# Moving two row normalisations of a fused attention and mixture-of-experts layer from VectorE to ScalarE

## The chip, the core and the metric

The kernel runs on one core of a Trainium2 chip. Its engines work from queues of their own and wait for each other by semaphores: TensorE (PE in the profile, PEld for its weight loads), VectorE (DVE), ScalarE (ACT), GpSimd (POOL) and SyncE (SP, which here only issues transfers). The metric is the device time of the whole kernel in microseconds (us), the median of several runs. Lower is better.

## What is computed

The input x is (2, 4096, 512) in float32: two batches of 4096 rows. The output is x plus an attention part plus a mixture-of-experts part, both fed with the normalised rows:

```python
x = L0_attn_x
xn = _layernorm(x, axis=-1)             # (x - mean) / sqrt(var + 1e-5)
x = x + attn(xn) + ffn(xn)

# attn: 64 compressed features per row, normalised again
c = (xn @ W_to_kv.T) @ W_compress.T
ch = (c - mean(c)) * rsqrt(var(c) + 1e-5) * ln_gamma + ln_beta
q, k, v = ...                           # from ch, with rotary tables
o = softmax(causal(q @ k.T / 8)) @ v
out = z @ W_to_kv + z @ W_out_res.T + b_out_res      # z = o @ W_comp2lat.T

# ffn: a shared expert for every row, and the best 2 of 16 experts per row
router_logits = xn @ router_w.T
shared = (silu(xn @ shared_gate_w) * (xn @ shared_up_w)) @ shared_down_w
```

## The kernel before

There are three phases. The first goes through the rows in 16 groups of 512 (four tiles of 128 rows each): statistics, normalisation, router logits, compressed features, the whole shared expert, the choice of experts, and every second group the projection to q, k and v. It ends near 740 us. The second gathers rows for their experts and multiplies them by the experts' weights. The third is the rest of the attention and the final sum. The change touches only the first phase.

The groups alternate between the batches: `seq` (L648) is half 0 of batch 0, half 0 of batch 1, half 1 of batch 0 and so on. A batch-1 group is followed by `project` (L608) for its half, whose work in the trace stands at the beginning of the stretch of the next batch-0 group.

For each group, in the order of the code:

- `front` (L372) belongs to the next group: it is called through `ahead` (L487, L724) in the middle of the current one. `load_x` (L360) loads 512 rows into one of two buffers. VectorE computes mean and variance (L376, L377), ScalarE the square root (L368), VectorE the reciprocal (L369), and L381 normalises four tiles of 128x512 into `xn`, which has a single buffer. POOL then adds the output bias to x in place (L384), so that the shared expert can be summed onto it.
- `group` (L450): TensorE multiplies the transposed rows into `lc`, a PSUM tile with 16 router logits and 64 compressed features per row (L458). VectorE takes the statistics of the features from PSUM (L466, L467), ScalarE the square root, and L471 normalises them into `cn` (128x64, four times). Then come the two best logits (L476, L477), the exponential for their weights (L481), and the store of `xn` with the weights in two extra columns (L488).
- The shared expert uses a scheme of seven products on quarters (`product`, L331) for gate and up together, and seven more for down. A product of gate and up fills one of two PSUM pairs. `sent(1)` is copied out by ScalarE (L517); the next ones, in the order 6, 2, 7, 5, 4, 3, are added onto running sums in SBUF by VectorE (L529, L530, L532, L534, L539, L541, L547), which frees the pair for the product after next. `gated` applies SiLU on ScalarE in place (L506) and multiplies on VectorE, both operands in SBUF (L507), into `hT`.
- The quarters of `hT` are combined for the down step (L546, L565 to L568), seven products follow in the order 1, 2, 4, 6, 7, 5, 3, and their sums go onto x (L581 to L601), which is stored (L602). Only then can the next load into that buffer start.
- `turn_x` (L430) transposes the next group's `xn` on TensorE, and ScalarE copies the result out (L447). `project` transposes `cn` and a copy of it with the batches swapped (`cns`, made by ScalarE in L621), applies gamma and beta (L626 on VectorE, L628 on ScalarE), and multiplies.

The order of instructions within each engine in this phase is not written out by hand. A planner sets it before the kernel runs, from the order of the code as a priority and from its own estimates of when inputs are ready. From the second phase on (L934) the order of TensorE, VectorE and ScalarE is that of the code.

The square root, the exponential and SiLU belong to different function tables of ScalarE. A change of table shows as an ACT_TABLE_LOAD on the line that needs it.

## Time and profile before

| | |
|---|---|
| median of three runs | 1941.44 us (1939.95, 1941.44, 1946.81) |
| profiled execution: time / span | 1946.36 / 1944.6 us |
| granted TensorE clock, mean | 0.99 |
| L381, VectorE, 64 instructions | 30.6 us, 542 ns each |
| L471, VectorE, 64 instructions | 17.6 us, 336 ns each |
| L384, POOL, 16 instructions | 76.0 us, 4752 ns each |
| ACT_TABLE_LOAD on L368, L506, L481 | 31, 23 and 16 times, 1283 ns each |

The profile is one execution, and a row of it gives a line of the code, the engine, the operation, output and input by name and shape, how often, the busy time and the mean duration. Behind a second bar stands the idle time of that engine just before these instructions and who ended it. In a timeline the two numbers ahead of the engine are start and duration in us from the start of the span, and brackets hold the idle time before. A busy engine isn't yet the one that sets the time: what sets it is who is waited for.

### The profile page before, as it was taken

What the parts mean: (1) busy time and instruction counts of PE and PEld (TensorE: products, weight loads), DVE (VectorE), ACT (ScalarE), POOL (GpSimd) and SP (SyncE); (2) the same over time, 40 slices, a digit from 0 to 9 for tenths busy, and PEclk for the clock granted to TensorE, in tenths of its full rate; (3) what the DMA queues carried; (4) which work ended last, traced back from release to release, by engine and by line L of the source; (5) the groups of instructions that cost most, each with busy time, mean ns of one, the idle gap of its engine ahead of it and who ended that gap; (6) DMA issues with size and microseconds to landing.
All of it is one profiled execution on the core that took longest, in us unless ns stands there. A gap on an engine that the chain in (4) does not pass through costs nothing. (4 is left out here: it accounts for less than half of the span.)

```text
span 1944.6 us, 33411 instructions
## 1 busy us (share of the span) xinstructions
PE 1866.0 (96%) x13010; PEld 1377.1 (71%) x13010; DVE 1060.9 (55%) x2882; ACT 648.2 (33%) x1097; POOL 575.6 (30%) x499
## 2 busy tenths in 40 slices
PE   7999999999999988999999999999999998999997
PEld 6888888888888875577777777777776674544544
DVE  8788778778787886632222222222223325777765
ACT  2222323233233324721111111111111454666664
POOL 2233433323242351011111111111111105555554
PEclk9999999999999999999999999999999999999998
DMA  6222223233222214067787887788776667888987
GB/s 238 66 77 66 76 66 94 71 94 102 66 77 66 77 49 153 2 196 262 271 301 250 271 285 275 270 277 283 272 278 236 241 221 192 206 206 208 217 208 183
DMA packets 219441, 342.52 MB, mean 176 GB/s; under 512 B 19204, under 2 KB 109952, under 8 KB 219280
## 3 DMA queue, kind: packets, MB, share of 16 engines
q1 hardware_dynamic: 167600, 234.09, 37.0%
q0 software_dynamic: 31696, 69.99, 14.3%
q10 hardware_dynamic: 19984, 36.25, 4.9%
q8 instruction: 105, 1.72, 0.4%
q14 instruction: 56, 0.46, 0.1%
HBM read 250.22 MB, written 90.05 MB: 175 GB/s over the span
## 5 line engine op out<-in xcount | busy, mean ns | idle before, releaser
L1043 PE MATMUL pg<-xt,wgu 128*128 128x256 f32 (+1 forms) x2816 | 496.1, 335 | 0.0
L1043 PEld LDWEIGHTS pg<-xt,wgu 128*128 128x128 f32 x2816 | 434.8, 191 | 43.0 <-issue 0.5
L985 POOL DMA_INDIRECT xg<-xn_d,table x137 | 130.6, 954 | 704.8 <-DVE sw L1025 553.2
L1049 DVE TENSOR_TENSOR eh<-esg,pg 128x512 f32<-128x512 f32 (+1 forms) x69 | 47.2, 683 | 396.6 <-ACT esg L1048 396.6
L1057 PE MATMUL py<-wdn,eh 128*128 128x512 f32 x548 | 247.1, 594 | 0.0
L1020 DVE COPY xt<-pxt 128x512 f32<-128x512 f32 x138 | 88.3, 681 | 176.7 <-PE pxt L1017 176.6
L1057 PEld LDWEIGHTS py<-wdn,eh 128*128 128x128 f32 x548 | 102.2, 190 | 106.6 <-issue 98.5
L812 DVE TENSOR_SCALAR_CACHE_REDUCE E<-s 128x512 f32<-128x512 f32 x224 | 144.7, 686 | 56.6 <-PE s L804 46.6
L1061 ACT ACTIVATE y<-py,sw 128x512 f32<-128x512 f32 x137 | 94.2, 688 | 231.4 <-PE py L1057 203.0
L1048 ACT ACTIVATE esg<-pg 128x512 f32<-128x512 f32 (+1 forms) x69 | 41.0, 594 | 383.1 <-PE pg L1043 292.2
L820 ACT ACTIVATE E<-E,nb 128x1024 f32<-128x1024 f32 (+7 forms) x160 | 160.8, 1008 | 22.6 <-DVE nb L815 22.5
L804 PE MATMUL s<-kT,qT 64*128 64x512 f32 (+3 forms) x576 | 145.0, 591 | 13.4 <-DVE E L812 8.7
L874 PE MATMUL oT<-eT,vv 128*64 128x256 f32 (+1 forms) x1088 | 145.7, 389 | 5.1 <-DVE qT L876 3.4
L423 POOL DMA_INDIRECT order_d<-tok,at_u x128 | 128.8, 1007 | 64.5 <-issue 36.1
L860 ACT COPY eT<-et 128x512 f32<-128x512 f32 x184 | 101.3, 587 | 111.8 <-PE et L854 84.4
L384 POOL TENSOR_TENSOR x<-x,b_bc 128x2048 f32<-128x2048 f32 x16 | 76.0, 4752 | 204.0 <-DVE xn L381 191.1
L874 PEld LDWEIGHTS oT<-eT,vv 128*64 128x64 f32 x1088 | 67.1, 137 | 94.2 <-ACT eT L860 32.1
L854 PEld LDWEIGHTS et<-ident,E 64*128 64x128 f32 x2112 | 83.5, 141 | 67.6 <-issue 47.8
L1135 POOL DMA_INDIRECT fac<-y_d,pos_all x64 | 99.8, 1560 | 72.8 <-DMA fac<-y_d,pos_all 56.8
L854 PE MATMUL et<-ident,E 64*128 64x64 f32 x2112 | 103.1, 232 | 14.0 <-ACT eT L860 6.3
L1135 POOL DMA_INDIRECT fyy<-y_d,pos_all x64 | 82.1, 1284 | 115.1 <-SPq L1090 54.6
L337 PE MATMUL gu<-xnT,Wg 128*128 128x256 f32 x384 | 99.5, 403 | 14.8 <-DVE gs L530 14.8
(246 smaller groups left out, 2728.1 us busy)
## 6 DMA issues: line engine op xcount, KB each, us to landing
wgu<-in_L_ffn_gate_w_dram SPq DMA_DIRECT2D x88, 512.0 KB, 5.5
wgu<-in_L_ffn_up_w_dram SPq DMA_DIRECT2D x88, 512.0 KB, 7.7
wdn<-in_L_ffn_down_w_dram SPq DMA_DIRECT2D x88, 512.0 KB, 4.7
y_d<-y ACTq DMA_DIRECT2D x137, 256.0 KB, 6.2
xn_d<-xn SPq DMA_DIRECT2D x16, 1028.0 KB, 7.1
x<-in_L_attn_x_dram SPq DMA_DIRECT2D x16, 1024.0 KB, 6.1
acc_d<-x SPq DMA_DIRECT2D x16, 1024.0 KB, 4.8
fac<-acc_d SPq DMA_DIRECT2D x64, 256.0 KB, 4.8
```

Of the source, the lines that this page charges most:

```text
L337: mm(out=o[:, r, :], lhsT=lhs[:, c, r * P:(r + 1) * P], rhs=rhs[:, c, :], start=c == 0, stop=c == 1)
L423: G.indirect_dma_start(out=order_d[n % 4], out_offset=bass.IndirectOffsetOnAxis(ap=at_u[:, i, k:k + 1], axis=0), in_=tok[:, g * 4 + i, k:k ...
L804: mm(out=sc[b][:, 0:w], lhsT=q[e, :], rhs=kT[c][e, 0:w], start=True, stop=True)
L812: V.tensor_scalar(dst, sc[b][:, 0:w], SCALE, None, ALU.mult, ALU.max, accum_out=m)
L820: S.activation(E, E, AF.Exp, bias=nb[:, b:b + 1], accum_out=sm[:, b, c:c + 1])
L854: tr(pt[h][:, o:o + H], rows[i][j // 8][e, b, (j % 8) * P:(j % 8 + 1) * P], ident[e, e])
L860: copy(dst[:, h:h + 3:2, :], pt[h].rearrange("p (u c) -> p u c", u=2))
L874: mm(out=o, lhsT=vv[j // 4][:, b, j % 4, :], rhs=e, start=(j == 0), stop=(j == n - 1))
L985: G.indirect_dma_start(out=x_n, out_offset=None, in_=xn_d, in_offset=bass.IndirectOffsetOnAxis(ap=table[:, n:n + 1], axis=0))
L1043: mm(out=pg[:, g, f, at_s], lhsT=weights[u][0][:, c, g * FE + f * P:g * FE + (f + 1) * P], rhs=x_u[:, c, :], start=(c == 0), stop=(c == 3))
L1057: mm(out=py[:, v, :], lhsT=hT[:, c, v * P:(v + 1) * P], rhs=weights[u][1][:, c, :], start=(c == 0), stop=(c == 1))
L1135: G.indirect_dma_start(out=y, out_offset=None, in_=y_d, in_offset=bass.IndirectOffsetOnAxis(ap=pos[k][:, j:j + 1], axis=0), compute_op=ALU ...
```

## The change

Both normalisations go from VectorE's "subtract the mean, multiply by the factor" to ScalarE's activation with the identity function, which computes factor times input plus addend. The factor is the same reciprocal as before. The addend, minus mean times factor, is a new small VectorE instruction for each group and each of the two normalisations, on 128x4 values, in a tile of its own with four buffers.

```diff
+            def minus_mean(mv, r, name):
+                m = p1.tile([P, 4], F32, tag="mmr", name=name, bufs=4)
+                V.scalar_tensor_tensor(m, mv[:, :, 0], -1.0, r, ALU.mult, ALU.mult)
+                return m
+
             def front(g, xt):
...
                 r = rstd_of(mv, 4, f"rx{g}")
                 xn = p1.tile([P, 4, D + TOPK], F32, tag="xn", name=f"xn{g}", bufs=1)
+                m = minus_mean(mv, r, f"mx{g}")
                 for i in range(4):
-                    V.tensor_scalar(xn[:, i, 0:D], xt[:, i, :], mv[:, i, 0:1], r[:, i:i + 1],
-                                    ALU.subtract, ALU.mult)
+                    S.activation(xn[:, i, 0:D], xt[:, i, :], AF.Identity, bias=m[:, i:i + 1], scale=r[:, i:i + 1])
...
                 r = rstd_of(mv, 4, f"rc{g}")
                 b = g // GPB
+                m = minus_mean(mv, r, f"mc{g}")
                 for i in range(4):
-                    V.tensor_scalar(cn[:, i, b, :], lc[:, i, NE:NE + DC], mv[:, i, 0:1], r[:, i:i + 1],
-                                    ALU.subtract, ALU.mult)
+                    S.activation(cn[:, i, b, :], lc[:, i, NE:NE + DC], AF.Identity, bias=m[:, i:i + 1], scale=r[:, i:i + 1])
```

## The prediction

> **What bounds the kernel now.** I read the page first, then busy time by stretches of 40 us, then the waits from 60 to 760 us (the first phase, which ends near 740 us), and last the timeline of two neighbouring groups. The page's totals, one stretch (us, then busy time of PE, PEld, DVE, ACT, POOL, the granted clock, DMA share, GB/s) and the waits ("total us, times, longest"):

> ```profile
> PE 1866.0 (96%) x13010; PEld 1377.1 (71%) x13010; DVE 1060.9 (55%) x2882; ACT 648.2 (33%) x1097; POOL 575.6 (30%) x499
> 440.00:480.00 40.00, 38.82 (x281) 32.68 (x280) 33.87 (x87) 13.95 (x21) 16.88 (x14) 1.00 0.22 68
> PE gu L337 <- DVE gs L530: 14.8, 7, 3.5
> PE gu L337 <- DVE gs L529: 4.2, 7, 1.0
> DVE st L376 <- DMA x<-in_L_attn_x_dram: 36.6, 14, 5.3
> ```

> The first phase is TensorE's: 38.8 of 40 us busy, VectorE 33.9, ScalarE 14.0. VectorE is heavily loaded, but what matters is how long TensorE waits for it. That is 14.8 + 4.2 = 19 us in the whole phase, always in one place: a product needs a PSUM pair that L529 or L530 frees by adding it away. The timeline of a batch-1 group (start, duration, engine) shows why L530 is late:

> ```profile
> 438.72 1.29 DVE L376 BATCH_NORM_STATS2 st<-x 128x6 f32<-128x512 f32 x2 [2.92 <-DMA x<-in_L_attn_x_dram]
> 441.32 1.19 DVE L530 TENSOR_TENSOR gs<-gs,gu 128x1024 f32<-128x1024 f32 x1
> 442.54 0.63 ACT L506 ACTIVATE gs<-gs 128x512 f32<-128x512 f32 x1 [8.43 <-DVE gs L530]
> 442.56 1.99 PE L337 MATMUL gu<-xnT,Wg 128*128 128x256 f32 x8 [1.18 <-DVE gs L530]
> 444.81 0.18 DVE L369 RECIPROCAL rx<-rx 128x4 f32<-128x4 f32 x1 [0.51 <-ACT rx L368]
> 445.03 1.91 DVE L381 TENSOR_SCALAR xn<-x,mv,rx 128x512 f32<-128x512 f32 x4
> 446.86 1.21 DVE L534 TENSOR_TENSOR gs<-gs,gu 128x1024 f32<-128x1024 f32 x1
> 447.02 4.55 POOL L384 TENSOR_TENSOR x<-x,b_bc 128x2048 f32<-128x2048 f32 x1 [15.40 <-DVE xn L381]
> 449.28 1.28 ACT L506 ACT_TABLE_LOAD   x1 [4.50 <-DVE gs L539]
> 451.24 1.49 DVE L507 TENSOR_TENSOR hT<-gs 128x512 f32<-128x512 f32 x2 [0.24 <-ACT gs L506]
> ```

> The statistics of the next rows stand in VectorE's queue ahead of L530 and wait 2.92 us for the load of x. That load waits for the same buffer's store (issued 427.00 after the last sum onto x, landed near 431.8; the load goes out at 431.90 and lands 6 to 7 us later). VectorE idles there; it isn't short of time. The normalisation itself (445.03) comes after L530, and in the batch-0 group before it (399.3 to 401.2) after L529 and L530 too.

> **What the change removes, adds and moves.** The rows (mean ns behind the bar) that carry the costs:

> ```profile
> L381 DVE TENSOR_SCALAR xn<-x,mv,rx 128x512 f32<-128x512 f32 x64 | 30.6, 542 | 7.6 <-DMA xn_d<-xn 7.3
> L471 DVE TENSOR_SCALAR cn<-plc,mvc,rc 128x64 f32<-128x64 f32 x64 | 17.6, 336 | 0.5
> L628 ACT ACTIVATE chT<-ptc,bet,gam 128x512 f32<-128x512 f32 x8 | 6.2, 778 | 9.8 <-PE ptc L623 9.8
> ```

> VectorE loses 30.6 + 17.6 = 48.2 us (1.91 and 1.10 us a group). It gains 32 small instructions for the addend; L415, the same kind on 128x8, takes 0.16 us: 5.1 us. Net -43 us of engine time, of which none is a wait of TensorE.

> ScalarE, the rows: L628 has the same function with both operands per row, from PSUM, at 0.778 us. The SiLU of L506 from SBUF takes 0.630, the copy L447 from PSUM 0.597, so I add 0.03 for the source: 0.81. Four L447 copies take 2.05 us where 4 x 0.597 = 2.39, so each after the first overlaps by 0.11: four in 2.9 us. The bounds are 2.05 us (plain copies) and 3.2 us (no overlap). The compressed rows, 128x64: the 128x4 square root with one operand per row takes 0.297; 60 more elements add 0.05 at the slope of L517 against L447 (1.00 - 0.597 us for 512); L628 against L447 gives 0.09 for an operand. That is 0.44, or 1.4 us for four. In all 16 x (2.9 + 1.4) = 69 us on an engine that is busy 14 of 40 us. [...] The time hides as follows. In the batch-1 group ScalarE sits idle from 444.79 to 449.28; reciprocal (445.0), addend (to 445.2) and four activations end near 448.2, ahead of the table load that waits for L539. In the batch-0 group it idles from 399.4 to 406.7; the rows end near 402.3. Transposes first need the rows near 421.9 and 464: cost 0, and if the cover is gone the 2.9 us stand ahead of a SiLU. For the compressed rows, cn would be ready near 431.5; if it goes ahead of the copy L517 (431.11), that copy ends at about 433.9 instead of 432.1, and product 2 needs its PSUM pair at 434.09 in batch 1 (covered) and at 392.4 in batch 0 (where the copy would end at 392.8: 0.4 us). I take it behind the copy: 0; bound 7 x 0.4 = 3 us. The store of xn waits for the exponential, which is ready before cn: SP's queue isn't moved. Table loads: L628 is issued today between functions of three tables without one on its line, so none is added; the bound, if every group loaded one more, is 16 x 1.28 us on ScalarE, inside its idle time.

> The wait of up to 1.5 us that L381 makes for the store of the old rows (7.3 us over 7 groups) passes to ScalarE; behind it is then a SiLU due 7 us later. Nothing of TensorE waits for it today.

> What moves is L384 on POOL, which overwrites x and so must now follow ScalarE: from 447.0 to about 448.3, ending at 452.9 instead of 451.6. Its own result isn't needed for 20 us. [...]

> The start: ScalarE can take the first rows from about 11.7 us (reciprocal 11.39), while VectorE begins only at 13.27 behind L314 and the evacuation L690. 11.7 + 2.9 = 14.6 against 15.18: -0.5 us. By the other bound (it starts when VectorE did) it is +1.2. The last group has no next rows; its cn, behind the copy L517 (to 697.1), would end near 698.5, before the transposes at 699.7: 0.

> **Sum.** -0.5 for the start, 0 to +3 for the compressed rows (I take +0.5), 0 for the rest: 0 us. The profiled execution has a span of 1944.6 us and a time of 1946.36, 4.9 above the median of the runs, 1941.44; I carry the difference over to the median and forecast 1942. About 0.5%, 9.7 us, is what a measurement of this kernel can tell from no change.

> The order within each engine's queue in this phase is the planner's; it may change with the cost of the moved work, and that I can't see in this trace. All rivals stand on it.

> **Rivals.** *Faster: the 19 us close.* With cn gone and rows off the queue the planner may put L529 or L530 ahead of the statistics. For it: those sums are ready at 392.4 and 439, before the statistics are done. Against: what holds them is the load of x, which the change doesn't touch. Half to all of 19 us, with some granted clock (0.91 to 0.96 in four stretches): about -12, 1929. Chance 0.18.

> [...] Chance 0.22.

> *Slower: a SiLU behind rows that wait for a store.* In batch 0 the rows wait for the old rows' store until 399.3; ahead of the SiLU they would hold it until 402.3, then table load and L507 in front of L532, which must end by 404.06 and would end near 406. 2 us in 7 groups: +14, 1956. Against: the SiLU's sum L530 is done before the reciprocal. Chance 0.10.

> *No change that can be told:* my forecast, chance 0.50.

> **Numbers.** Faster by over 0.5% 0.18, within 0.5% 0.51, slower 0.31 (nearly all of the two slower cases). The range runs from 1929 to 1963: it holds half of the faster case, the second slower case and the lock in 7 groups with some in the others; the far half of the one (0.09) and the lock in most groups (0.08) are left out. My forecast's own range is 1936 to 1948: the 3 us bounds above, and the spread of the runs (6.9 us).

> **What would show it.** Right: VectorE's busy time some 43 us lower, ScalarE's some 69 higher, the waits of products for L529 and L530 still near 19 us, stretches of 40 us still with about 39 of TensorE. [...] A SiLU held shows as L507 waiting for L506 (11.0 us in 27 waits now). Closed gaps show as the L530 row gone. Wrong I am if the planner's order is another, first of all the order of the statistics, L529 and L530.

## The result and the profile after

The changed kernel takes 1972.45 us (median of six runs), the kernel before 1942.55 us beside it: a ratio of 1.0156, 95% interval 1.0138 to 1.0173. It is 30 us slower, where the prediction said 1942 us and a range of 1929 to 1963 us. Of the two slower rivals, the SiLU behind the rows at 1956 us and VectorE's product held by POOL's addition at 1958 us, both are found in the trace, in the same seven groups.

The profiled execution took 1971.71 us. From the page of the changed kernel, and from its waits between 60 and 780 us (engine, line, what it waited for: total us, times, longest us). Five lines were added, so L381 of before is now L387, L506 and L507 are L511 and L512, the sums L529, L530 and L539 are L534, L535 and L544, and the bias addition L384 is L389.

```profile
PE 1872.1 (95%) x13010; PEld 1379.2 (70%) x13010; DVE 1045.0 (53%) x2786; ACT 712.7 (36%) x1225; POOL 568.2 (29%) x499
...
L389 POOL TENSOR_TENSOR x<-x,b_bc 128x2048 f32<-128x2048 f32 x16 | 72.4, 4527 | 236.8 <-ACT xn L387 224.0
```

```profile
PE gu L337 <- DVE gs L544: 16.4, 7, 2.8
PE gu L337 <- DVE gs L535: 12.6, 7, 3.4
PE gu L337 <- DVE gs L534: 8.7, 7, 2.9
...
ACT xn L387 <- DMA xn_d<-xn: 25.0, 7, 3.8
...
DVE hT L512 <- ACT gs L511: 26.8, 30, 2.8
```

TensorE's waits for sums grew from 19 to 37.7 us. One row is new: the wait for L544 (product 5's second sum, behind which the pair is free for product 3), once in each of the seven batch-0 groups behind the first step. L534 rose from 4.2 to 8.7, L535 changed little. Two other waits have grown with it: ScalarE stands idle for 25.0 us ahead of the normalised rows until the store of the old rows has landed (VectorE for 7.3 us), and `hT` waits 26.8 us for the SiLU (11.0). VectorE's wait for the load of x grew too, from 36.6 to 47.1 us.

Where it lies is seen from the time between the first transpositions of two groups. A step that holds a batch-0 group took 45.55 us in the mean and now takes 49.96 us (seven steps; the first step, with the start in it, is left out); one with a batch-1 group took 43.92 and takes 43.26 us. The last group's first transposition moves from 686.87 to 714.37 us, so the whole loss is there by then. The sums of TensorE's busy time over these 15 steps, of the kernel before and of the changed one:

```profile
sum 673.00, PE 653.29 PEld 556.83 DVE 533.43 ACT 203.35 POOL 232.87; mean PE 43.55 PEld 37.12 DVE 35.56 ACT 13.56 POOL 15.52
```

```profile
sum 700.14, PE 661.61 PEld 560.25 DVE 517.75 ACT 265.94 POOL 227.65; mean PE 44.11 PEld 37.35 DVE 34.52 ACT 17.73 POOL 15.18
```

The steps are 27.1 us longer. Idle time of TensorE is 18.8 us of that (38.5 against 19.7), and 8.3 us are busy time: the same matmuls took longer. About half of the 8.3 us is the granted clock: TensorE worked 13.0 us at a clock of 0.50 in these steps before and 21.8 us after. In the kernel before, 8 matmuls take the 3.00 us from 353.0 at a clock of 0.50 and 16 the 3.00 us from 356.5 at 1.00, so half of the difference is lost, 4.4 us. For the rest the traces give only an estimate: a step at full clock is busy for 40.61 us without a wait (in the kernel before with late statistics, at the end of the experiments) and for 40.88 us with one (in the kernel before, 151.13 to 193.22), so seven more waits make some 1.9 us. The last 2 us are open.

The timeline of one batch-0 group of the changed kernel shows the chain (start, duration, engine):

```profile
405.68 0.17 DVE L369 RECIPROCAL rx<-rx 128x4 f32<-128x4 f32 x1
...
405.96 1.22 DVE L535 TENSOR_TENSOR gs<-gs,gu 128x1024 f32<-128x1024 f32 x1
...
408.44 2.93 ACT L387 ACTIVATE xn<-x,mx,rx 128x512 f32<-128x512 f32 x4 [3.47 <-DMA xn_d<-xn]
...
411.39 1.28 ACT L511 ACT_TABLE_LOAD   x1
411.45 4.53 POOL L389 TENSOR_TENSOR x<-x,b_bc 128x2048 f32<-128x2048 f32 x1 [11.84 <-ACT xn L387]
...
412.68 0.63 ACT L511 ACTIVATE gs<-gs 128x512 f32<-128x512 f32 x1
...
413.35 3.18 DVE L512 TENSOR_TENSOR hT<-gs 128x512 f32<-128x512 f32 x1 [2.55 <-ACT gs L511]
...
416.45 1.21 DVE L539 TENSOR_TENSOR gs<-gs,gu 128x1024 f32<-128x1024 f32 x1
417.58 1.21 DVE L544 TENSOR_TENSOR gs<-gs,gu 128x1024 f32<-128x1024 f32 x1
...
418.93 1.97 PE L337 MATMUL gu<-xnT,Wg_s 128*128 128x256 f32 x8 [2.49 <-DVE gs L544]
```

It is read from top to bottom. The SiLU's input is ready at 407.2 (L535). But on ScalarE the rows stand ahead of it, and ScalarE is idle for 3.47 us until the store of the old rows has landed (the addend is there at 406.04, so the store alone holds the rows for 2.4 us). Then come 2.93 us of rows and 1.28 us of table load, and the SiLU runs at 412.68, 5.5 us after its input was there. By now the end of the rows has also released POOL's bias addition at 411.45. VectorE's product L512 comes at 413.35, in the middle of it, and takes 3.18 us instead of 0.69: it ends 0.55 us behind the addition (416.53 and 415.98). This hold is called the lock here, and the expectations below call it the port or the port lock; what the two engines share isn't shown by any run. Two sums stand behind it on VectorE, and TensorE waits 2.49 us for the second.

In the kernel before, the same place has another order: on ScalarE the table load comes at 397.43 and the SiLU at 398.73, while the rows wait for the store in VectorE's queue:

```profile
397.43 1.28 ACT L506 ACT_TABLE_LOAD   x1
398.73 0.63 ACT L506 ACTIVATE gs<-gs 128x512 f32<-128x512 f32 x1
...
399.27 1.91 DVE L381 TENSOR_SCALAR xn<-x,mv,rx 128x512 f32<-128x512 f32 x4 [0.86 <-DMA xn_d<-xn]
```

### The profile page after: what moved, and what is told of

Same layout as the page of the kernel before. It is cut to its first block, busy times and chain, and to the rows that moved or that the text cites. A ratio compares the mean times of both kernels' runs of the same rounds, so it can differ in the third digit from the quotient of the medians.

```text
span 1969.9 us, 33487 instructions
## 1 busy us (share of the span) xinstructions
PE 1872.1 (95%) x13010; PEld 1379.2 (70%) x13010; DVE 1045.0 (53%) x2786; ACT 712.7 (36%) x1225; POOL 568.2 (29%) x499
## 5 line engine op out<-in xcount | busy, mean ns | idle before, releaser
L389 POOL TENSOR_TENSOR x<-x,b_bc 128x2048 f32<-128x2048 f32 x16 | 72.4, 4527 | 236.8 <-ACT xn L387 224.0
L337 PE MATMUL gu<-xnT,Wg 128*128 128x256 f32 x384 | 99.1, 402 | 12.6 <-DVE gs L535 12.6
```

Of the source, the lines that this page charges most:

```text
L337: mm(out=o[:, r, :], lhsT=lhs[:, c, r * P:(r + 1) * P], rhs=rhs[:, c, :], start=c == 0, stop=c == 1)
```

## The experiments

Twelve kernels ran, four at a time on one chip. The kernel before took 1955.14 us on the first of these chips, 1960.82 us on the second and 1944.09 us on the third; so only ratios to the runs of before on the same chip are compared, and "of before" below means these. Steps and waits come from one profile of each kernel and differ a little between chips too: a batch-0 step of the change took 49.96 us, and 50.41 us on the second of these chips. My theory after the result was: rows ahead of the SiLU on ScalarE, then VectorE's product held by POOL's addition, both needed. The rivals: the wait for the store alone, the lock alone, ScalarE's added work as such, and one half of the change by itself.

**The SiLU ahead of the rows.** The rows and the bias addition are listed behind the first SiLU of a group; all else is as changed.

```diff
-                for i in range(4):
-                    S.activation(xn[:, i, 0:D], xt[:, i, :], AF.Identity, bias=m[:, i:i + 1], scale=r[:, i:i + 1])
+                def rows():
+                    for i in range(4):
+                        S.activation(xn[:, i, 0:D], xt[:, i, :], AF.Identity, bias=m[:, i:i + 1], scale=r[:, i:i + 1])
+                    G.tensor_tensor(xt, xt, b_bc.unsqueeze(1).to_broadcast([P, 4, D]), ALU.add)
 
-                G.tensor_tensor(xt, xt, b_bc.unsqueeze(1).to_broadcast([P, 4, D]), ALU.add)
+                if g == seq[0]:
+                    rows()
+                else:
+                    held_back.append(rows)
...
-                    gated(k1, 0, 0)
+                    with tc.issue_after(gated(k1, 0, 0).ins):
+                        held_back.pop()()
```

> The changed kernel, but the activations of the rows are queued behind the first SiLU of the group on ScalarE (a queue order, no wait). Theory (two delays in series in the batch-0 groups: the SiLU stands behind rows that wait 3.6 us for the store of the old rows, and then POOL's addition of the bias holds the port when L512 comes): the SiLU is early again, L512 of 3.2 us is gone, product 3 waits no longer for L544 (16.4 us in 7 waits now). About 17 us less than the changed kernel, 1955. Rival (the port lock alone): L512 is still held somewhere, since POOL still starts when the rows end, 1968 to 1972. Rival (more work on ScalarE as such, or VectorE's new order): no gain, 1972.

Measured: a ratio of 1.0026 (1.0006 to 1.0045). Steps with a batch-0 group take 46.52 us, against 49.96 in the change and 45.55 before, and TensorE's waits for sums in the first phase are those for the first two, as before:

```profile
PE gu L337 <- DVE gs L542: 14.2, 7, 3.8
PE gu L337 <- DVE gs L541: 9.3, 7, 1.6
```

(L541 and L542 are L534 and L535 of the change.) The row for product 5's sum is gone, and the product that was held takes its usual time in the same group:

```profile
399.94 0.69 DVE L518 TENSOR_TENSOR hT<-gs 128x512 f32<-128x512 f32 x1 [0.69 <-ACT gs L517]
```

1.3 of the 1.56 per cent hang on this order, more than the 17 us I had expected. The same work is on the same engines. But two things were moved together, the rows and, with them, POOL's addition.

**The store early.** The rows are stored as soon as they are made, and the two weight columns from a small tile of their own, so that the next rows find their buffer free.

```diff
+                nc.sync.dma_start(
+                    out=xn_d[g * 512:(g + 1) * 512, 0:D].rearrange("(i p) d -> p i d", p=P), in_=xn
+                )
                 return (xn,)
...
-                V.tensor_copy(xn[:, :, D:D + 1], ww)
-                V.tensor_tensor(xn[:, :, D + 1:D + 2], dl, ww, ALU.mult)
+                wt = p1.tile([P, 4, TOPK], F32, tag="wt", name=f"wt{g}")
+                V.tensor_copy(wt[:, :, 0:1], ww)
+                V.tensor_tensor(wt[:, :, 1:2], dl, ww, ALU.mult)
                 nxt = ahead()
                 nc.sync.dma_start(
-                    out=xn_d[g * 512:(g + 1) * 512, :].rearrange("(i p) d -> p i d", p=P), in_=xn
+                    out=xn_d[g * 512:(g + 1) * 512, D:].rearrange("(i p) d -> p i d", p=P), in_=wt
                 )
```

> The changed kernel, but the rows are stored as soon as they are normalised, and the two weight columns go out of a small tile of their own, so that the next rows never wait for a store. Theory: ScalarE's 25 us of waits for the store are gone, rows, SiLU and POOL's addition all come 2 to 3 us earlier in batch 0; L512 is still held by the port, but ends 2.2 us earlier, so that product 3 waits some 0.3 us: about 15 us less than the changed kernel, 1957. Rival (the port lock alone): POOL shifts with the rows, the block stays, 1968 to 1972. Rival (ScalarE's work as such): 1972.

Measured: 1.0089 (1.0057 to 1.0122), so more than half of the loss is left; in the profiled execution, the slowest of the four, a batch-0 step takes 50.25 us, no less than in the change. The rows no longer wait for the store, but stand ahead of the SiLU as before, and the product is held all the same. From this kernel's timeline of a batch-0 group:

```profile
403.53 2.93 ACT L387 ACTIVATE xn<-x,mx,rx 128x512 f32<-128x512 f32 x4 [1.10 <-DVE mx L374]
...
406.53 4.52 POOL L389 TENSOR_TENSOR x<-x,b_bc 128x2048 f32<-128x2048 f32 x1 [10.12 <-ACT xn L387]
...
408.43 3.17 DVE L516 TENSOR_TENSOR hT<-gs 128x512 f32<-128x512 f32 x1 [3.80 <-ACT gs L515]
...
412.79 3.55 PE L337 MATMUL gu<-xs,Wg 128*128 128x256 f32 x8 [2.35 <-DVE gs L541]
```

The wait for the store is not needed for the loss: rows and table load alone put the SiLU into the bias addition. The reading is not clean, because the planner here also put the held product ahead of product 7's sum (L541), so that TensorE waits one product earlier than in the change.

**Without the bias addition, and its control.** The edit is one line, made once in the changed kernel and once in the kernel before. The output then lacks b_out_res. The order on TensorE, VectorE and ScalarE stays as it was in each.

```diff
-                G.tensor_tensor(xt, xt, b_bc.unsqueeze(1).to_broadcast([P, 4, D]), ALU.add)
```

> The changed kernel without POOL's addition of the output bias (its output lacks b_out_res); the order of TensorE, VectorE and ScalarE is the same. Theory: L512 is 0.7 us everywhere; the SiLU is as late as before in batch 0, but L512 then ends near 414.0 in the group where it ended at 416.5, and product 3 is just in time: about 17 us less than the changed kernel, 1955. Rival (the wait for the store alone makes the loss): L512 still waits 2.5 us for the SiLU and product 3 for it, 1968 or more. Rival (ScalarE's work as such): 1972.

> Control: the kernel before without POOL's addition of the output bias (its output lacks b_out_res), order of the other engines unchanged. Theory: POOL's addition holds hardly any VectorE instruction there except one of 5 us in the first group, off TensorE's path: 1940 to 1943, no change. If the addition cost something in general (the port, or POOL's queue), this is faster too, and the gain of its removal from the changed kernel must be taken less this.

Measured: the change without it 1.0005 (0.9984 to 1.0026), the kernel before without it 0.9985 (0.9969 to 1.0). The distance between the two is 0.2% where the change itself makes 1.5%. In the change without it the SiLU is as late as ever: ScalarE waits 25.6 us for the store ahead of the rows, and `hT` waits 2.47 us for the SiLU in the batch-0 group below. But `hT` then takes 0.69 us, and product 5's sum (L543 here) is waited for 1.5 us in all instead of 16.4:

```profile
403.63 0.69 DVE L511 TENSOR_TENSOR hT<-gs 128x512 f32<-128x512 f32 x1 [2.47 <-ACT gs L510]
...
PE gu L337 <- DVE gs L534: 14.4, 7, 3.8
PE gu L337 <- DVE gs L533: 7.0, 7, 1.5
...
PE gu L337 <- DVE gs L543: 1.5, 4, 0.6
```

So a late SiLU alone costs nearly nothing, and the lock decides. Together with the first experiment: the late SiLU does its harm by bringing the product into the lock.

**Each half alone.** The rows on ScalarE with the compressed rows on VectorE, and the other way round, beside the change once more on the same chip. The edit is the corresponding part of the change taken back.

> The changed kernel once more, beside the halves of it on one chip: ratio to the kernel before 1.0156 as measured (1.0138 to 1.0173).

> Only the rows move to ScalarE, the compressed rows stay on VectorE. In the queue written for this kernel the SiLU of batch 0 stands ahead of the rows, as the reciprocal stands behind L535 on VectorE. Theory (the loss is the SiLU behind the rows plus the port): nearly all of the loss is absent, ratio 1.000 to 1.004, L512 of over 2 us only in batch 1, where it is covered. Rival (the rows' work on ScalarE, or POOL's later addition, costs as such): 1.010 or more.

> Only the compressed rows move. VectorE is freed of 1.1 us ahead of the statistics, and the planner then puts all four statistics and the reciprocal ahead of L535, and L534 behind all four statistics; the rows stay on VectorE. Theory: no port block, no late SiLU; L534 some 0.7 us later in 7 batch-0 groups (4.2 us of waits before, 8.7 in the changed kernel): ratio 1.002 to 1.004. Rival (the activations on 128x64, at 0.39 to 0.41 us, delay the copy L522 and with it TensorE in every group): 1.006 or more.

Measured: the change 1.0149 (1.0127 to 1.0171), the rows alone 1.0011 (0.9996 to 1.0026), the compressed rows alone 1.0003 (0.9986 to 1.0019). The two halves don't add up to the whole, and the compressed rows alone cost less than the 0.2 to 0.4% that I had expected. With the rows alone, ScalarE's timeline in a batch-0 group has the old order:

```profile
402.51 1.28 ACT L511 ACT_TABLE_LOAD   x1
403.81 0.63 ACT L511 ACTIVATE gs<-gs 128x512 f32<-128x512 f32 x1
404.61 2.93 ACT L387 ACTIVATE xn<-x,mx,rx 128x512 f32<-128x512 f32 x4 [0.18 <-DMA xn_d<-xn]
```

The SiLU runs while the rows would have to wait for the store anyway. Which half is moved matters only through the order that comes of it.

**The converse.** The kernel with the rows alone costs 0.1%. If one queue place makes the loss, forcing it there must bring the loss without the compressed rows.

```diff
-                    S.activation(xn[:, i, 0:D], xt[:, i, :], AF.Identity, bias=m[:, i:i + 1], scale=r[:, i:i + 1])
+                    last_row[0] = S.activation(xn[:, i, 0:D], xt[:, i, :], AF.Identity, bias=m[:, i:i + 1], scale=r[:, i:i + 1])
...
-                    gated(k1, 0, 0)
+                    if g < GPB and g != seq[0]:
+                        with tc.issue_after(last_row[0].ins):
+                            gated(k1, 0, 0)
+                    else:
+                        gated(k1, 0, 0)
```

> The rows on ScalarE and the compressed rows on VectorE, as in the run with the rows alone (ratio 1.001), but in the batch-0 groups the first SiLU is listed behind the four rows, as it stood by itself in the changed kernel. One queue place is changed. Theory (rows ahead of the SiLU, which then is late and meets the port held by GpSimd's bias addition): the batch-0 groups lengthen from 46.4 us to 49 to 50 us, VectorE's transposing product is held for about 3 us there, TensorE waits 2 to 3 us more for a sum behind it, and the ratio is 1.009 to 1.014. Rival (the loss needs both halves because of the work that both together put on ScalarE): 46.4 us and 1.001 as without the edit.

Measured: 1.0117 (1.0097 to 1.0138), a batch-0 step of 49.65 us, and the new wait is back (L549 here is product 5's sum, L536 product 2's):

```profile
PE gu L337 <- DVE gs L549: 15.5, 7, 2.5
PE gu L337 <- DVE gs L536: 15.1, 7, 3.7
```

In its timeline the statistics and the sums L535 and L536 stand in the same sequence on VectorE as with the rows alone. The SiLU is late, the product is held, and product 7's sum now stands ahead of the product, as in the change:

```profile
415.54 4.52 POOL L389 TENSOR_TENSOR x<-x,b_bc 128x2048 f32<-128x2048 f32 x1 [10.86 <-ACT xn L387]
...
417.44 3.17 DVE L513 TENSOR_TENSOR hT<-gs 128x512 f32<-128x512 f32 x1 [2.10 <-ACT gs L512]
```

The rival (ScalarE's added work) asked for 1.001. It falls. With one place in ScalarE's queue 1.1 of the 1.5 per cent are back; why not all of it isn't shown.

**The statistics late.** The order can also be mended at its other end. The load of the next group's x is left where it was, but `front`, its statistics and all that follows, is listed behind product 2's sum, in every group but the last, so that the statistics no longer stand ahead of the two sums that TensorE waits for. Made of the changed kernel (twice), of the kernel before, and of the change with the SiLU ahead of the rows.

```diff
-                    return (t, *front(seq[n + 1], t))
+                    return lambda: (t, *front(seq[n + 1], t))
...
-                    V.tensor_tensor(k1, k1, sent(2), ALU.add)
+                    with tc.issue_after(V.tensor_tensor(k1, k1, sent(2), ALU.add).ins):
+                        nxt = nxt()
                     gated(k1, 0, 0)
```

> The changed kernel, with the statistics of the next rows queued behind L535 on VectorE, so that the sums L534 and L535 no longer stand behind statistics that wait for the load of x. On ScalarE the first SiLU of a group is then ahead of the rows too, and the store of the old rows goes out earlier, since its two columns no longer stand behind a statistic. Theory: the waits of TensorE for L534 and L535 (21 us in the changed kernel, 19 before) go, and the late SiLU with them: ratio 0.990 to 0.994, faster than both kernels. Rival (the load of x bounds the group through the rows themselves, or VectorE gets too late for L537 to L544): the waits only move to the later products, 0.998 to 1.006.

> The kernel before, with one thing changed: the statistics of the next rows, with all that follows from them, are listed behind the first sum of the products of an even group (product 2's), so that no statistic stands ahead of a sum that TensorE waits for. No ScalarE rows. Theory (the loss is one of order: statistics ahead of the sums, and rows ahead of the first SiLU; moving the rows is by itself worth almost nothing): the two sum waits of some 19 us in the batch-0 groups go, and the ratio is 0.985 to 0.992, within 0.003 of the same order with ScalarE rows. Rival 1 (43 us less on VectorE is worth something once the order is good): 0.993 to 0.998 here, so that the move gains. Rival 2 (the held product of VectorE costs even there): 0.980 to 0.984 here.

> The change with the late statistics a second time, on the chip of the kernel that has the late statistics alone: 0.985 to 0.989 as the first time; only its distance from that kernel is asked for.

> The change with the late statistics and, besides, the rows and the bias addition listed behind the first SiLU in every group. Theory (with the statistics late, the rows stand behind that SiLU or near it anyway): within 0.003 of the change with late statistics, so 0.984 to 0.990. Rival (a held product still costs there): 0.980 to 0.983.

Measured: the change with late statistics 0.987 (0.985 to 0.9889), and the second time, on the chip of the others, 0.9891 (0.9873 to 0.9908); the kernel before with late statistics 0.9872 (0.9854 to 0.989); with the SiLU ahead besides, 0.9906 (0.9888 to 0.9924), where I had expected 0.984 to 0.990. The first is better than the 0.990 to 0.994 that I had put down. The kernel before with late statistics, 1918.46 us, is 1.3% faster than the kernel before and 2.8% faster than the change (0.9872 / 1.0156 = 0.972). Two of its 15 steps, and their sum:

```profile
357.79:402.48 44.69, 44.69 (x310) 38.17 (x309) 36.51 (x93) 14.79 (x21) 16.34 (x15) 1.00 0.24 83
402.48:443.09 40.61, 40.61 (x269) 35.55 (x269) 33.25 (x90) 13.58 (x19) 13.44 (x13) 1.00 0.23 79
...
sum 645.14, PE 644.47 PEld 554.95 DVE 531.79 ACT 210.73 POOL 224.57; mean PE 42.96 PEld 37.00 DVE 35.45 ACT 14.05 POOL 14.97
```

In a row of steps come the stretch, its length, then busy times of PE, PEld, VectorE, ScalarE and POOL, the granted clock, DMA share and GB/s. TensorE is without a gap, and the clock is 1.00: in 15 steps it is idle for 0.7 us (645.14 - 644.47). In this frame the normalisations on ScalarE bring nothing: 1923.46 us against 1918.46 on the same chip, four runs each whose ranges (1921.61 to 1927.70, 1916.34 to 1920.51) don't meet. VectorE's products `hT` are held there too, 72.9 us in all against 42.5 us, and nearly all of it is covered; the SiLU's place changes nothing, as the theory had it.

## Why the prediction was wrong, step by step

- **Which step failed.** It is the step "In the batch-0 group it idles from 399.4 to 406.7; the rows end near 402.3", and the sentence "Against: the SiLU's sum L530 is done before the reciprocal" that held the rival of the SiLU behind the rows to a chance of 0.10. Both took the order on ScalarE of before, SiLU first, as given, and added the rows behind it. The order is an output of the planner. In the changed kernel the reciprocal (405.68) stands ahead of product 2's sum (405.96) and the rows ahead of the SiLU. What it led to is the new wait for product 5's sum, 16.4 us in seven groups, put at 0 in the sum. The converse experiment shows that this one place is enough for most of the loss (1.0011 to 1.0117), and the first experiment that without it most of the loss is gone (1.0026).
- **A SiLU behind rows that wait for a store, priced at 2 us a group.** The mechanism is the one described: a wait for the store, the rows, the table load. Its price by itself was too high, not too low: without the bias addition the same late SiLU costs 0.2%, no more than the measurement tells.
- **The lock, put into batch 1.** The rival waited for rows that fall behind the next SiLU there. The lock struck in batch 0 instead, which I had left out: I had POOL end near 406.9 there (rows to 402.3 and some 4.5 us of addition) and L507 come at 407.4, and that too was worked out with the SiLU ahead of the rows. The general rule behind that rival, and behind the 0 that the sum has for a hold, is shown by no run. What the runs showed in its place is this product held by this addition: 3.18 us against 0.69 in batch 0, and in batch 1, in five of the seven groups, 2.40 us, where I had 1.6 us of hold on 0.68, and TensorE doesn't wait there.

```profile
369.64 4.53 POOL L389 TENSOR_TENSOR x<-x,b_bc 128x2048 f32<-128x2048 f32 x1 [17.12 <-ACT xn L387]
...
372.32 2.40 DVE L512 TENSOR_TENSOR hT<-gs 128x512 f32<-128x512 f32 x1
```

- **Two rivals kept apart.** I gave the rows behind the SiLU and the SiLU behind the rows a chance each and a price each, 14 to 16 us. A late SiLU brings a late product, and the late product is just what runs into the addition that the same rows release. One cause moves both ends towards each other, and the sum of the two prices, 30 us, is what was measured. That the two figures add up so well is chance: the late SiLU by itself cost next to nothing, and some 4 us of the loss are the granted clock, which neither price held.
- **Engine time.** VectorE's -43 us was right as a count: its busy time fell by only 15.9 us, because `hT` went from 44.5 to 70.4 us, 25.9 us of which are held time. ScalarE's rise of 64.5 us (predicted 69) is as worked out: four rows in 2.93 us (2.9), four compressed rows in 1.29 us (1.4). Table loads stay at 31, 23 and 16. Added up over both engines, the engine times of the prediction make 26 us (69 + 5 - 48), and that sum explains little: with a good order the move costs 5 us (one pair of kernels on one chip), not 26, and with a bad one 30 us.
- **Compressed rows, start.** Half a microsecond was taken for the one; alone the compressed rows cost 0.03% with an interval of -0.14 to +0.19%. The first transposition moved from 13.87 to 14.23 us, +0.36 where I had -0.5.
- **The load of x, which I held against the faster rival.** "What holds them is the load of x, which the change doesn't touch" is true of the wait, and yet only because statistics stood ahead of sums. Listed behind them, the same load costs TensorE nothing, and 25 us are gained. The half of the faster rival that I named in a clause ("with some granted clock") is large: the kernel before lost 19.7 us of idle time over 15 steps, and with late statistics 27.9 us went (673.00 to 645.14, one profile each): 19.0 us of idle time and 8.8 us of busy time, of which 6.5 us are the 13.0 us that had run at half clock.

Why both halves are needed is shown in part. With the compressed rows alone the reciprocal stands ahead of product 2's sum already:

```profile
400.40 0.17 DVE L369 RECIPROCAL rx<-rx 128x4 f32<-128x4 f32 x1
400.58 1.22 DVE L535 TENSOR_TENSOR gs<-gs,gu 128x1024 f32<-128x1024 f32 x1
```

With the rows alone it stands behind that sum, and the SiLU ahead of the rows, both in all seven batch-0 groups. So the one half brings the reciprocal forward on VectorE, and the other puts the rows into ScalarE's queue, where they come ahead of the SiLU. That the planner does it by its estimates of when inputs are ready is my reading; nothing was tried with the planner itself.

## What to carry to other kernels

Moving an instruction from a busy engine to an idle one moves it in somebody's queue, and if a planner sets the queues, the whole order around it may come out differently; cost such a change once with the present order and once with the moved work ahead of the first thing that waits on that engine. When two mishaps share a cause, price them together: a chain that makes one end late and releases a long operation that holds this end is one case and not two. Look for what is queued ahead of the sum that TensorE waits for before looking for time on the engine: here three lines of order gave 1.3%, and taking 43 us of work off VectorE gave nothing.

## What the runs showed of the hardware

**The lock is exact and selective.** Each held product ended 0.55 us behind the end of the bias addition (415.98 and 416.53 us in the change, 420.06 and 420.61 with the SiLU forced back, 411.05 and 411.60 with the early store; 0.55 or 0.56 us for each of the 17 held products in the traces of before and of the change), so the wait is the remainder of POOL's instruction. Not `hT` alone is held. In the first group of the kernel before, the addition meets a subtraction between quarters of a weight, which takes 5.00 us where the same line took 0.68 us before:

```profile
11.51 0.68 DVE L314 TENSOR_TENSOR Wg_s<-Wg 128x512 f32<-128x512 f32 x1
...
17.15 4.92 POOL L384 TENSOR_TENSOR x<-x,b_bc 128x2048 f32<-128x2048 f32 x1 [12.90 <-DMA pro<-in_L_attn_W_q_comp_dram]
...
17.63 5.00 DVE L314 TENSOR_TENSOR Wu_s<-Wu 128x512 f32<-128x512 f32 x1
```

It goes the other way round too: where VectorE's product comes first, as in the kernel before from 401.10 to 401.78, POOL's addition, from 401.26, takes 4.93 us instead of 4.53. The sums that read one operand from PSUM weren't held: with the rows alone, POOL adds from 407.62 to 412.17, and inside it VectorE runs two such sums at their usual length:

```profile
407.62 4.55 POOL L389 TENSOR_TENSOR x<-x,b_bc 128x2048 f32<-128x2048 f32 x1 [12.40 <-ACT xn L387]
...
409.34 1.22 DVE L539 TENSOR_TENSOR gs<-gs,gu 128x1024 f32<-128x1024 f32 x1 [2.23 <-PE gu L337]
410.48 1.21 DVE L544 TENSOR_TENSOR gs<-gs,gu 128x1024 f32<-128x1024 f32 x1
```

**Waits cost TensorE its clock, and not by their length alone.** Behind some waits the granted clock is half for a while: in the kernel before it is 0.50 from 353.0 to 356.4 us. In the changed kernel, five microseconds after waits for a sum of 2.49, 2.76 and 3.38 us (the clock is the third number from the end):

```profile
418.90:423.90 5.00, 4.97 (x25) 4.48 (x26) 4.26 (x7) 1.24 (x2) 0.00 (x0) 1.00 0.01 3
510.10:515.10 5.00, 5.00 (x16) 4.11 (x17) 3.11 (x4) 1.18 (x2) 0.00 (x0) 0.66 0.00 0
549.30:554.30 5.00, 5.00 (x12) 4.01 (x13) 2.08 (x5) 4.53 (x7) 0.00 (x0) 0.50 0.00 0
```

```profile
349.59:353.00 3.41, 1.51 (x8) 1.00 (x7) 3.41 (x10) 0.17 (x1) 0.00 (x0) 1.00 0.37 136
527.05:530.47 3.42, 1.64 (x8) 1.10 (x6) 2.10 (x6) 0.00 (x0) 0.00 (x0) 1.00 0.95 362
530.47:533.88 3.41, 1.67 (x8) 1.49 (x9) 3.41 (x6) 1.67 (x2) 0.00 (x0) 1.00 0.01 5
```

Idle for 1.90 us of its 3.41, the first window is followed by half clock; idle for 1.78 and 1.75 us, the two others are not. In these two traces 389 windows lie at full clock between the first and the last group's transpositions. By the recorded matmuls, TensorE was idle for 1.90 us or more in nine of them, and half clock followed each time; it was idle for 1.82 us or less in the 380 others, and half clock followed none. An estimate from these windows, for this kernel: a wait costs its own length, and if about 1.9 us or more of it fall into one window, another 1.7 us (half of 3.41). It can be more: behind the waits of 3.38 us (changed kernel) and 3.11 us (before), the next window began idle as well, half clock lasted 6.8 us, and 5.5 and 6.2 us of it were work. The edges don't fall at the same place in every trace: the first one of the grid lies 2.74 us into the span of the kernel before and 1.83 us into that of the change.
